# q and k of a two-layer graph network made for two pairs of batches at once

## The chip, the cores and the metric

The kernel runs on one core of one Trainium2 chip. The metric is the device time of one execution in microseconds, the median of several runs. One further execution is recorded by the hardware profiler; all views of the profile shown here come from it.

## The reference

x has 128 batches of 128 nodes with 512 features; adj is one 128 x 128 matrix of zeros and ones. Two layers follow each other, each with a residual and a normalisation of rows. All is float32.

```python
# layer 0: attention with 8 heads of 64, masked by adj
q, k, v = x @ Wq + bq, x @ Wk + bk, x @ Wv + bv
scores = einsum('bqhd,bkhd->bhqk', q, k) / 8 + (1 - adj) * -1e9
out = einsum('bhqk,bkhd->bqhd', softmax(scores), v)
x = layernorm(x + out @ Wo + bo)
# layer 1: graph attention
h = x @ W
e = leaky_relu((h @ a1)[:, :, None] + (h @ a2)[:, None, :], 0.2) * adj
x = layernorm(x + elu(softmax(e) @ h + beta * h))
```

## The kernel before

**Groups and products.** Two batches make a group, 64 groups in all (G = 2, NG = 64). Each of the five products with a 512 x 512 weight (q, k, v, w for Wo, h for W) is made for a whole group by a Strassen-like scheme: the weight and the pair of batches are cut into blocks of 256, seven block products replace eight, and sums of blocks are formed before and after. `product(name, g, n)` issues block product n (1 to 7); `weight_sum` forms the sums of weight blocks once, at the start; `block_sum(name, g, n)` forms the four differences of x blocks on POOL, for each group. Products 1, 6, 5 and 3 accumulate in one region of PSUM, product 2 has its own, and 7 and 4 share a third. `take_part` moves a region out of PSUM, `add_block` adds one on VectorE. A product that continues a region must wait until the region was read by the step before it: 4 waits for the add of 7.

**Shapes.** In v, w and h a block of x is stationary and 256 columns of the weight move (line 298). In q and k (line 304) the weight block is stationary and 128 columns, the nodes of one batch, move; so a q or k product is 4 matmuls of 128 columns and a v, w or h product 2 of 256. Each float32 matmul has two records in the profile, so these are 8 and 4 records.

**One group's way.** `fetch_blocks` loads x in blocks of 32 rows, `turn_x` transposes it on VectorE into xT (once for each batch of the group), then `block_sum`, the products of q, k and v, `scores` on TensorE, `mask` and `row_max` on VectorE, `exps` and `normalise` on ScalarE. `attn_write` and `attn_read` carry the weights of attention through DRAM in blocks, `turn_attn` transposes them on VectorE, `attend` multiplies with v, `attend_evict` adds v's bias. w's products follow, with x (read again by `fetch_x`, with bo added by `residual` on POOL) as residual. The second layer is alike but smaller: `wa_column` computes W a for both halves of a on VectorE, once at the start; `edge`, `leaky`, `edge_exp` and `weights` make its attention; `aggregate` and h's products end it, with `elu_max`, `elu_exp` and `elu_sum`, and `norm_f` and `store`.

**Order.** Nothing is left to a scheduler. Every call is a piece with a place, a number near its due time in microseconds from a plan. All pieces are sorted by place and issued in that order, so that each engine's queue and SP's DMA queue have a fixed order and wait in it. `rows(g)` holds one group's places; group g adds g * STEP. The table `other` has places of their own for the first and last groups, and `last_rows` has the end, in which the last group's work is cut in halves (`end_product`, `end_max`, `end_sum`, `end_stats`) and w is made plainly. Engines wait by semaphores for what they need, so a place is an order and no fixed time.

**Start.** x of group 0, then Wq, Wk and Wv are loaded through SP. `load_later` issues five small loads on POOL: bv, beta, the halves of a (each spread over 128 partitions), bo. `keep_busy` runs matmuls on the identity until work arrives. `wa_column` needs W and a.

**Buffers.** PSUM is a pool of eight tiles of one bank. xT and the differences tx have two buffers (groups alternate), qT and kT one, v two.

Of the kernel before, what the change touches and what calls it, by code (L numbers as in the profile page):

```python
# [13 lines left out]
P = 128  # L14
# [4 lines left out]
STEP = 36.678  # L19
# [3 lines left out]
def gnn_two_layers(  # L23
# [54 lines left out]
    def load_blocks(g):  # L78
        t = grp.tile([P, G, 4, P], F32, tag="xb", name=f"xblk_{g}", bufs=1)
        for a in range(4):  # L80
            (nc.scalar if g == 0 and a >= 2 else nc.sync).dma_start(
                out=t[a * Q : (a + 1) * Q].rearrange("r t b d -> r (t b) d"),
                in_=x[g * G : (g + 1) * G, :, a * P : (a + 1) * P].rearrange(
                    "t (b r) d -> r (t b) d", r=Q
                ),
            )
        return t
# [25 lines left out]
    xblk, xn = {0: load_blocks(0)}, {}  # L113
# [23 lines left out]
    keep_busy(15, "early")  # L137
# [92 lines left out]
    xT, right, tx, qT, kT, vb, y, hp, main, side, oT, zT, xr = ({} for _ in range(13))  # L230
    BIAS = {"q": bq_c, "k": bk_c}
    OUT = {"q": qT, "k": kT, "v": vb, "w": y, "h": hp}

    def turn_x(g, t):
        if t == 0:
            xT[g] = grp.tile([P, NC, G * N], F32, tag="xT", name=f"xT_{g}")
        nc.vector.transpose(  # L237
            xT[g][:, :, t * N : (t + 1) * N].rearrange("p m (b r) -> p b m r", r=Q),
            xblk[g][:, t].rearrange("p b (c m) -> p b m c", c=Q),
        )  # L240

    def block_sum(name, g, n):

        if name == "x":
            b11, b12 = xT[g][:, :2, :N], xT[g][:, :2, N:]
            b21, b22 = xT[g][:, 2:, :N], xT[g][:, 2:, N:]
        else:
            src = oT if name == "w" else zT
            b11, b12 = src[g * G][:, :2], src[g * G + 1][:, :2]
            b21, b22 = src[g * G][:, 2:], src[g * G + 1][:, 2:]  # L250
        if (name, g) not in tx:
            tx[name, g] = grp.tile(
                [P, 4, 2, N], F32, tag=f"t{name}", name=f"t{name}_{g}", bufs=2 if name == "x" else 1
            )
        t1, t2, t3, t4 = (tx[name, g][:, i] for i in range(4))
        to, a, b = {1: (t1, b12, b11), 2: (t2, b22, t1), 3: (t3, b22, b12), 4: (t4, b21, t2)}[n]
        nc.gpsimd.tensor_tensor(to, a, b, ALU.subtract)  # L257
        right[name, g] = {1: b11, 2: b21, 3: b22, 4: t4, 5: t1, 6: t2, 7: t3}

    def first_blocks(name, g):  # L260

        if (name, g) in right:
            return right[name, g]
        if name == "x":
            return {1: xT[g][:, :2, :N], 2: xT[g][:, 2:, :N]}
        src = oT if name == "w" else zT
        return {1: src[g * G][:, :2], 2: src[g * G][:, 2:]}

    def region(name, g, n):

        if n in (7, 4):
            return side[name, g]
        return main[name, g][:, 1 if n == 2 else 0]

    def product(name, g, n):
        first = False
        if n == 1:
            main[name, g] = ps_mm.tile([P, 2, HF], F32, tag="mm", name=f"p{name}_{g}")
            first = True
        if n == 7:  # L280
            if name == "k":
                side["k", g] = side["qk", g][:, 1]
            else:
                t = ps_mm.tile([P, 2, HF], F32, tag="mm", name=f"e{name}_{g}")
                side["qk", g] = t
                side[name, g] = t[:, 0]
                first = True


        out = region(name, g, n)  # L290
# [4 lines left out]
        b = first_blocks(name if name in "wh" else "x", g)[n]  # L295
        if name in "vwh":
            for c in range(2):
                nc.tensor.matmul(  # L298
                    out, b[:, c, :], a[:, c, :], start=first and c == 0, stop=(c == 1), skip_group_check=True,
                )  # L300
        else:
            for m in range(2):
                for c in range(2):
                    nc.tensor.matmul(  # L304
                        out[:, m * N : (m + 1) * N], a[:, c, m * P : (m + 1) * P], b[:, c, :],
# [4 lines left out]
    def block(name, g, i, j):  # L310

        out = OUT[name]
        if name in "qk":
            if g not in out:
                out[g] = grp.tile([P, NC, G * N], F32, tag=name, name=f"{name}T_{g}", bufs=1)
            return out[g][:, 2 * i : 2 * i + 2, j * N : (j + 1) * N]
        return whole(name, g * G + j)[:, i * HF : (i + 1) * HF]

    def whole(name, b):
        out = OUT[name]  # L320
        if b not in out:
            out[b] = wk2.tile([P, D], F32, tag=name, name=f"{name}_{b}")
# [18 lines left out]
    def take_part(name, g, n, i, j):  # L341
# [8 lines left out]
        else:  # L350
            for m in range(2):
                nc.scalar.activation(  # L352
                    dst[:, m, :], src[:, m * N : (m + 1) * N], AF.Identity,
# [3 lines left out]
    def add_block(name, g, n, i, j):  # L357

        src, dst = region(name, g, n), block(name, g, i, j)
        if name in "qk":  # L360
            src = src.rearrange("p (m n) -> p m n", m=2)
# [5 lines left out]
    def scores(b):  # L367
# [4 lines left out]
        rows = slice(i * N, (i + 1) * N)  # L372
        for m in range(HP):
            for j in range(2):
                feats = slice(j * HD, (j + 1) * HD)
                nc.tensor.matmul(  # L376
                    psc[b][j][:, m, :], qT[g][feats, m, rows], kT[g][feats, m, rows],
# [360 lines left out]
    def rows(g):  # L738

        b0, b1 = g * G, g * G + 1  # L740
        return (
            (-44.347, fetch_blocks, g), (-35.5, turn_x, g, 0), (-35.24, turn_x, g, 1),
            (-33.234, block_sum, "x", g, 1), (-29.664, block_sum, "x", g, 2),
            (-28.037, block_sum, "x", g, 3), (-27.486, block_sum, "x", g, 4),
            (-24.602, product, "q", g, 1), (-22.912, take_part, "q", g, 1, 0, 0),
            (-17.846, product, "k", g, 1), (-17.044, take_part, "k", g, 1, 0, 0),
            (-16.821, product, "q", g, 2), (-16.581, product, "q", g, 6),
            (-13.839, product, "k", g, 6), (-13.188, product, "k", g, 2),
            (-12.987, take_part, "q", g, 6, 1, 0), (-12.001, product, "q", g, 7),
            (-11.879, add_block, "q", g, 2, 0, 0), (-11.237, product, "k", g, 7),  # L750
            (-10.614, product, "q", g, 5), (-10.426, add_block, "k", g, 2, 0, 0),
            (-9.421, take_part, "k", g, 6, 1, 0), (-8.361, take_part, "q", g, 5, 1, 1),
            (-7.18, product, "k", g, 5), (-5.626, fetch_x, b0),
            (-5.405, take_part, "k", g, 5, 1, 1), (-5.039, product, "q", g, 3),
            (-4.941, add_block, "q", g, 7, 1, 1), (-4.893, add_block, "k", g, 7, 1, 1),
            (-4.838, product, "k", g, 3), (-4.757, residual, b0),
            (-3.456, take_part, "k", g, 3, 0, 1), (-3.441, take_part, "q", g, 3, 0, 1),
            (-0.228, product, "q", g, 4), (0.123, fetch_x, b1), (0.161, product, "k", g, 4),
            (0.517, add_block, "k", g, 4, 1, 0), (1.111, add_block, "q", g, 4, 1, 0),
            (2.487, scores, b0), (3.199, scores, b1), (4.193, mask, b0, 0),  # L760
            (4.492, product, "v", g, 1), (4.517, mask, b0, 1), (4.517, row_max, b0),
            (4.641, mask, b1, 0), (5.302, take_part, "v", g, 1, 0, 0), (5.86, exps, b0, 0),
            (6.834, residual, b1), (7.227, product, "v", g, 6), (7.65, product, "v", g, 2),
            (7.788, exps, b0, 1), (8.282, mask, b1, 1), (8.312, exps, b0, 2),
            (8.356, row_max, b1), (9.38, exps, b0, 3), (9.64, product, "v", g, 7),
            (9.91, add_block, "v", g, 2, 0, 0), (10.078, take_part, "v", g, 6, 1, 0),
            (10.336, row_inv, b0), (10.432, normalise, b0, 0), (10.446, normalise, b0, 1),
            (10.513, normalise, b0, 2), (11.118, product, "v", g, 5), (12.165, normalise, b0, 3),
            (12.283, exps, b1, 0), (12.823, attn_write, b0), (16.179, exps, b1, 1),
            (17.177, exps, b1, 2), (17.937, exps, b1, 3), (18.213, row_inv, b1),  # L770
            (20.003, normalise, b1, 0), (20.463, normalise, b1, 1), (21.094, normalise, b1, 2),
            (21.248, normalise, b1, 3), (21.546, attn_read, b0), (21.948, turn_attn, b0, 0),
            (22.433, attn_write, b1), (23.511, take_part, "v", g, 5, 1, 1),
            (24.964, product, "v", g, 3), (26.507, turn_attn, b0, 1),
            (27.155, add_block, "v", g, 7, 1, 1), (27.181, attn_read, b1),
            (30.486, product, "v", g, 4), (31.193, take_part, "v", g, 3, 0, 1),
            (31.929, turn_attn, b1, 0), (32.334, turn_attn, b1, 1),
            (32.982, add_block, "v", g, 4, 1, 0), (36.883, attend, b1), (38.699, attend, b0),
            (39.543, attend_evict, b0), (39.643, attend_evict, b1),
            (40.299, block_sum, "w", g, 1), (40.441, block_sum, "w", g, 2),  # L780
            (41.662, block_sum, "w", g, 3), (42.036, product, "w", g, 1),
            (42.978, product, "w", g, 2), (44, take_part, "w", g, 1, 0, 0),
            (44.174, add_block, "w", g, 2, 0, 0), (45.529, block_sum, "w", g, 4),
            (46.326, product, "w", g, 6), (46.362, product, "w", g, 7),
            (47.112, take_part, "w", g, 6, 1, 0), (47.797, product, "w", g, 5),
            (49.563, take_part, "w", g, 5, 1, 1), (50.272, add_block, "w", g, 7, 1, 1),
# [385 lines left out]
```

## Time and profile before

| | |
|---|---|
| Median of 3 runs | 2380.74 us (2379.07 to 2380.99) |
| The profiled execution | 2381.36 us, its span 2379.6 us, mean granted clock 0.998 |
| TensorE, loads of stationary blocks | 2353.9 us, 2177.3 us (99%, 91% of the span) |
| VectorE, ScalarE, POOL | 1960.5, 1589.5, 867.7 us (82%, 67%, 36%) |
| DMA | 269.83 MB, 113 GB/s on average |
| q and k products (line 304) | 7168 of 17702 matmul records |

A row of the page or of a group list gives line, engine, operation, tiles, count, busy time and mean duration. A row of the timeline gives start and length of a run of like instructions; in brackets stands the idle time before it with what ended it. A row of the stretch table gives a stretch, its length, the busy time of TensorE, its weight loads, VectorE, ScalarE and POOL with the number of instructions, the granted clock, the DMA engines' share and GB/s. Matmuls overlap, so their durations are longer than the distances of their starts. Times are from the span's start.

### The profile page before, as it was taken

To read this page: it belongs to the slowest core of one execution; us is meant where nothing else is said; L and a number is where in the kernel's file an instruction comes from. 1 tells how busy PE (TensorE), PEld (TensorE's weight loads), DVE (VectorE), ACT (ScalarE), POOL (GpSimd) and SP (SyncE) were. 2 spreads that over 40 slices of the span, in tenths; PEclk is the share of its full clock that TensorE was granted. 3 is DMA by queue.
4 is the path that set the end of the run, shared out by engine and by line. 5 is a ranking of instruction groups with operands and counts; after the bars stand their busy time and mean duration, and the time that the engine had idled before them with its cause. 6 is when DMAs were issued, how large, how long until landed. Compare 5 with 4: busy or idle time off the path is not lost.

```text
span 2379.6 us, 50867 instructions
## 1 busy us (share of the span) xinstructions
PE 2353.9 (99%) x17702; PEld 2177.3 (91%) x17702; DVE 1960.5 (82%) x4390; ACT 1589.5 (67%) x5762; POOL 867.7 (36%) x1047
## 2 busy tenths in 40 slices
PE   8999999999999999999999999999999999999997
PEld 7999899999999999999999999999999999999986
DVE  6787788888888888888888888888888888888887
ACT  4675666766766667667666676676666766766765
POOL 6243333433433334334333333343343333433432
PEclk9999999999999999999999999999999999999999
DMA  6333334334333343343433433424434334333432
GB/s 192 107 92 119 111 107 125 95 118 128 97 119 116 105 122 103 109 134 92 120 119 103 122 108 109 127 91 121 123 102 118 110 109 125 96 117 124 114 115 73
DMA packets 256193, 269.83 MB, mean 113 GB/s; under 512 B 57456, under 2 KB 204912, under 8 KB 255552
## 3 DMA queue, kind: packets, MB, share of 16 engines
q1 hardware_dynamic: 254992, 265.45, 37.1%
q8 instruction: 140, 2.29, 0.4%
q0 software_dynamic: 400, 0.86, 0.1%
q14 instruction: 117, 0.96, 0.1%
q10 hardware_dynamic: 544, 0.26, 0.0%
HBM read 157.62 MB, written 108.85 MB: 112 GB/s over the span
## 4 chain that ended last, share of the span: by engine, by line
PE 95%; DMA 2%; DVE 1%; ACT 1%; issue 0%; SPq 0%; POOLq 0%; POOL 0%; ACTq 0%; DVEq 0%
PE pk L304 12%; PE pq L304 12%; PE pv L298 12%; PE ph L298 11%; PE pw L298 11%; PE eq L304 9%; PE psc L376 5%; PE po L451 5%; PE pz L639 5%; PE eh L298 4%; PE ew L298 4%; PE ev L298 4%; DMA w_sb<-in_L_gnn_W_dram 1%; DMA wk_sb<-in_L_gnn_Wk_dram 0%; DMA scr<-sb 0%
## 5 line engine op out<-in xcount | busy, mean ns | idle before, releaser
L432 POOL TENSOR_TENSOR x<-x,bo_b_in 128x512 f32<-128x512 f32 x128 | 163.3, 1277 | 858.6 <-DMA x<-in_x_dram 858.6
L398 ACT ACTIVATE s<-s,nmax 128x128 f32<-128x128 f32 x1024 | 396.9, 396 | 58.3 <-DVE nmax L392 58.2
L412 ACT ACTIVATE sb<-s,rinv 128x128 f32<-128x128 f32 x1024 | 325.2, 392 | 0.4 <-DVE rinv L405 0.4
L352 ACT ACTIVATE kT<-pk,bk_c 128x128 f32<-128x128 f32 x512 | 159.7, 363 | 204.3 <-PE pk L304 146.2
L352 ACT ACTIVATE qT<-pq,bq_c 128x128 f32<-128x128 f32 x512 | 160.1, 367 | 156.7 <-PE pq L304 156.7
L502 DVE SCALAR_TENSOR_TENSOR ya<-w,wa_row 128x512 f32<-128x512 f32 x256 | 223.9, 874 | 4.4
L398 ACT ACTIVATION_READ_ACCUMULATOR s<-s,nmax 128x1 f32 x1024 | 199.2, 195 | 0.0
L463 ACT ACTIVATE oT<-po,bv_c 128x128 f32<-128x128 f32 x512 | 139.1, 382 | 80.2 <-PE po L451 80.1
L349 DVE TENSOR_TENSOR w<-pw,x 128x256 f32<-128x256 f32 x252 | 106.4, 422 | 99.8 <-PE pw L298 94.0
L441 DVE STREAM_TRANSPOSE attnT<-ab 128x512 f32<-128x512 f32 x256 | 172.6, 693 | 7.5 <-DMA ab<-scr 7.2
L384 DVE SCALAR_TENSOR_TENSOR s<-psc,amask 128x512 f32<-128x512 f32 x256 | 168.7, 681 | 0.8 <-PE psc L376 0.8
L392 DVE TENSOR_REDUCE nmax<-s 128x8 f32<-128x1024 f32 x128 | 156.1, 1220 | 4.4
L346 ACT COPY h<-ph 128x256 f32<-128x256 f32 x252 | 93.7, 372 | 94.9 <-PE ph L298 94.7
L346 ACT COPY v<-pv 128x256 f32<-128x256 f32 x256 | 94.4, 369 | 86.4 <-PE pv L298 59.9
L237 DVE STREAM_TRANSPOSE xT<-xblk 128x512 f32<-128x512 f32 x128 | 139.7, 1110 | 6.2 <-DMA xblk<-in_x_dram 6.2
L257 POOL TENSOR_TENSOR tx<-xT 128x256 f32<-128x256 f32 x128 | 95.6, 748 | 124.3 <-PE psc L376 104.3
L654 DVE SCALAR_TENSOR_TENSOR u<-h,x 128x512 f32<-128x512 f32 x126 | 87.1, 691 | 63.7 <-ACT h L346 61.6
L304 PE MATMUL pq<-xT,wq_sb 128*128 128x128 f32 x1024 | 135.1, 275 | 3.0 <-DMA wq_sb<-in_L_gnn_Wq_dram 3.0
L304 PE MATMUL pk<-xT,wk_sb 128*128 128x128 f32 x1024 | 135.9, 277 | 2.1 <-DMA wk_sb<-in_L_gnn_Wk_dram 2.1
L298 PE MATMUL pv<-wv_sb,xT 128*128 128x256 f32 x512 | 137.5, 392 | 0.0
L304 PEld LDWEIGHTS pk<-xT,wk_sb 128*128 128x128 f32 x1024 | 130.2, 193 | 5.5 <-DMA wk_sb<-in_L_gnn_Wk_dram 2.3
L304 PEld LDWEIGHTS pq<-xT,wq_sb 128*128 128x128 f32 x1024 | 129.3, 192 | 6.4 <-issue 3.2
(677 smaller groups left out, 6349.8 us busy)
## 6 DMA issues: line engine op xcount, KB each, us to landing
scr<-sb SPq DMA_DIRECT2D x128, 512.0 KB
ab<-scr SPq DMA_DIRECT2D x512, 128.0 KB
x<-in_x_dram SPq DMA_DIRECT2D x128, 256.0 KB
xblk<-in_x_dram SPq DMA_DIRECT2D x254, 128.0 KB
out_dram<-u SPq DMA_DIRECT2D x126, 256.0 KB
pb<-s2d SPq DMA_DIRECT2D x62, 128.0 KB
attd<-att SPq DMA_DIRECT2D x62, 128.0 KB
ab<-attd SPq DMA_DIRECT2D x248, 32.0 KB
```

Source lines behind the costliest of these rows:

```text
L237: nc.vector.transpose(xT[g][:, :, t * N : (t + 1) * N].rearrange("p m (b r) -> p b m r", r=Q), xblk[g][:, t].rearrange("p b (c m) -> p b m ...
L298: nc.tensor.matmul(out, b[:, c, :], a[:, c, :], start=first and c == 0, stop=(c == 1), skip_group_check=True,)
L304: nc.tensor.matmul(out[:, m * N : (m + 1) * N], a[:, c, m * P : (m + 1) * P], b[:, c, :], start=first and m == 0 and c == 0, stop=(c == 1) ...
L346: nc.scalar.copy(dst, src)
L352: nc.scalar.activation(dst[:, m, :], src[:, m * N : (m + 1) * N], AF.Identity, bias=BIAS[name][:, 2 * i + m : 2 * i + m + 1],)
L384: nc.vector.scalar_tensor_tensor(s_t[b][:, j * HP : (j + 1) * HP, :], psc[b][j], SCALE, amask.rearrange("p (o n) -> p o n", o=1).broadcast ...
L392: nc.vector.tensor_reduce(nmax[b], s_t[b], AX.X, ALU.max, negate=True)
L398: nc.scalar.activation(s_t[b][:, h, :], s_t[b][:, h, :], AF.Exp, bias=nmax[b][:, h : h + 1], accum_out=rsum[b][:, h : h + 1],)
L412: nc.scalar.mul(sb[b][:, :, h, :], s_t[b][:, h, :].rearrange("p (b c) -> p b c", c=Q), rinv[b][:, h : h + 1],)
L432: nc.gpsimd.tensor_tensor(xr[b], xr[b], later["bo"], ALU.add)
L441: nc.vector.transpose(attnT[b].rearrange("p h (a r) -> p a h r", r=Q)[:, rows], ab[b].rearrange("p a (h c) -> p a h c", c=Q)[:, rows],)
L502: nc.vector.scalar_tensor_tensor(z, y[b], 1.0, wa_row[j], ALU.mult, ALU.mult, accum_out=s12[g][:, i, j : j + 1])
```

## The change

q and k are made for two groups (a pair of groups, four batches) by one set of products. xT and the differences of all pairs lie in two fixed tiles, `xT_all` and `xs_all`, in which the even and the odd group are side by side; `x_blocks(None)` gives blocks with 256 columns, `x_blocks(0)` and `x_blocks(1)` the 128 of one group for v. `product` for q and k moves 256 columns and has a PSUM tile for each of its three regions; q's and k's evictions and adds are of that width, and `scores` takes its group's part. v has four buffers.

```diff
-STEP = 36.678
+STEP = 72.624
...
     def load_blocks(g):
-        t = grp.tile([P, G, 4, P], F32, tag="xb", name=f"xblk_{g}", bufs=1)
+        if g == 1:
+
+            t = wk2.tile([P, H, N], F32, tag="attnT", name="xblk_1")
+            t = t.rearrange("p (t b) d -> p t b d", t=G)
+        else:
+            t = grp.tile([P, G, 4, P], F32, tag="xb", name=f"xblk_{g}", bufs=1)
...
-    xblk, xn = {0: load_blocks(0)}, {}
+    xblk, xn = {0: load_blocks(0), 1: load_blocks(1)}, {}
...
-    keep_busy(15, "early")
+    keep_busy(20, "early")
...
+    xT_all = cpool.tile([P, NC, G, 2, N], F32, tag="xT", name="xT")
+    xs_all = cpool.tile([P, 4, 2, 2, N], F32, tag="tx", name="tx")
+
     def turn_x(g, t):
-        if t == 0:
-            xT[g] = grp.tile([P, NC, G * N], F32, tag="xT", name=f"xT_{g}")
         nc.vector.transpose(
-            xT[g][:, :, t * N : (t + 1) * N].rearrange("p m (b r) -> p b m r", r=Q),
+            xT_all[:, :, t, g % 2, :].rearrange("p m (b r) -> p b m r", r=Q),
...
+    def x_blocks(slots):
+        s = slice(slots, slots + 1) if isinstance(slots, int) else slice(0, 2)
+        b = [xT_all[:, 2 * h : 2 * h + 2, j, s] for h in range(2) for j in range(G)]
+        t = [xs_all[:, i, :, s] for i in range(4)]
+        b11, b12, b21, b22, t1, t2, t3, t4 = (a.rearrange("p c s n -> p c (s n)") for a in b + t)
+        return b11, b12, b21, b22, (t1, t2, t3, t4)
...
+    def factor(name, g, n):
+
+        if name in "qkv":
+            b11, b12, b21, b22, (t1, t2, t3, t4) = x_blocks(g % 2 if name == "v" else None)
+            return {1: b11, 2: b21, 3: b22, 4: t4, 5: t1, 6: t2, 7: t3}[n]
...
+        if name in "qk":
+            return (two if n == 2 else main)[name, g]
...
-                        out[:, m * N : (m + 1) * N], a[:, c, m * P : (m + 1) * P], b[:, c, :],
+                        out[:, m, :], a[:, c, m * P : (m + 1) * P], b[:, c, :],
...
-                out[g] = grp.tile([P, NC, G * N], F32, tag=name, name=f"{name}T_{g}", bufs=1)
-            return out[g][:, 2 * i : 2 * i + 2, j * N : (j + 1) * N]
+                out[g] = grp.tile([P, NC, G, 2, N], F32, tag=name, name=f"{name}T_{g}", bufs=1)
+            return out[g][:, 2 * i : 2 * i + 2, j].rearrange("p m s n -> p m (s n)")
...
-        rows = slice(i * N, (i + 1) * N)
+        qs, ks = (t[g - g % 2][:, :, i, g % 2, :] for t in (qT, kT))
```

All places are new: `rows` has one list for even groups, which also makes q and k for the pair, and one for odd groups, which has only v; a pair g // 2 adds (g // 2) * STEP. Of the new lists the parts that the steps below speak of (the whole has some 160 pieces a group):

```python
# even group
(-29.134, product, "k", g, 1), (-28.828, product, "q", g, 1), (-28.51, product, "k", g, 2),
...
(0.747, scores, b0), (0.767, scores, b1),
...
(19.288, product, "v", g, 3),
...
(25.91, normalise, b1, 3),
...
(31.237, attn_write, b1), (33.268, attn_read, b0), (33.385, attn_read, b1), (33.851, turn_attn, b0, 0),
(34.469, turn_attn, b0, 1), (34.976, turn_attn, b1, 0), (35.624, turn_attn, b1, 1),
(36.826, attend, b0), (36.846, attend, b1),
# x of the next even group: places -48.877 and -42.022 of turn_x, one STEP on 23.7 and 30.6
# odd group
(-38.159, fetch_blocks, g), (-36.754, turn_x, g, 0), (-34.832, turn_x, g, 1),
...
(34.39, product, "v", g, 4),
...
(61.056, normalise, b1, 3),
```

At the start the order changes as well. On POOL `load_later` moves from ahead of all work to behind v's weight sums, and on VectorE `wa_column` stands between the adds of product 2 and those of product 7:

```diff
-    at(0.583, load_later)
-    at(5.685, load_k_and_v)
+    at(-1.685, load_k_and_v)
...
+    at(11.013, weight_sum, "v", 3, nc.gpsimd)
+    at(12.293, weight_sum, "v", 1, nc.gpsimd)
+    at(13.573, weight_sum, "v", 2, nc.gpsimd)
+    at(14.853, weight_sum, "v", 4, nc.gpsimd)
+    at(16.133, load_later)
+    at(16.198, wa_column, 1, 1)
+    at(16.928, wa_column, 0, 2)
+    at(17.658, wa_column, 0, 3)
+    at(18.388, wa_column, 0, 1)
+    at(19.118, wa_column, 1, 2)
+    at(19.848, wa_column, 1, 3)
```

There the first pair's products on TensorE stand in the order q 1, 7, 2, k 1, 7, 6, 2, q 6, k 5, q 5, k 3, q 3, q 4, k 4, v 1, scores. VectorE has k's add 7 at place 20.578, q's add 7 at 21.963, q's add 4 at 26.008 and k's at 27.743. SP has x of batches 0 and 1, Wo and W1 (the second layer's weight) behind Wv; before, W1 stood ahead of Wo. At the end `last_rows` gives the last two batches' four `end_product` calls first and then, behind them on VectorE, all of `end_max`, `end_sum` and `end_stats`.

## Prediction

> **What bounds the kernel now.** I read the page's busy times, then the stretch table of two groups, TensorE's timeline, and last the start and the end.
>
> ```profile
> PE 2353.9 (99%) x17702; PEld 2177.3 (91%) x17702; DVE 1960.5 (82%) x4390; ACT 1589.5 (67%) x5762; POOL 867.7 (36%) x1047
> ...
> 1036.57:1073.07 36.50, 36.50 (x278) 33.92 (x277) 30.44 (x71) 24.80 (x90) 13.27 (x16) 1.00 0.37 113
> 1073.07:1109.57 36.50, 36.50 (x278) 33.92 (x276) 30.40 (x70) 24.81 (x90) 13.28 (x16) 1.00 0.37 113
> ```
>
> Two stretches from scores to scores are both 36.50 us with TensorE busy throughout, while VectorE has 6 us free and ScalarE 12. Now the timeline inside one:
>
> ```profile
> 1042.11 1.03 PE L298 MATMUL pv<-wv_sb,xT 128*128 128x256 f32 x4
> ...
> 1046.43 1.03 PE L298 MATMUL pw<-wo_sb,tw 128*128 128x256 f32 x4
> ...
> 1067.51 1.05 PE L304 MATMUL pq<-xT,s_q 128*128 128x128 f32 x8
> ...
> 1070.19 1.06 PE L304 MATMUL eq<-tx,wk_sb 128*128 128x128 f32 x8
> ```
>
> Starts, not durations, give the price. Five products of 4 records with 256 columns lie between 1042.11 and 1046.43: 0.864 us each, 216 ns a record. Three products of 8 records with 128 columns lie between 1067.51 and 1070.19: 0.893 us each, 111.6 ns a record. A column is dearer in the narrow form, and TensorE has no gap that anything else could fill. Ahead of this steady part stands a start of some 30 us, behind it an end that waits on chains.
>
> **What the skill says.** "Perfetto Trace Analysis", section Identifying the Most-Contended Engine, warns that matmul busy share says little of headroom; hence starts. "TensorE: Matmul & The Clock Gate", section Back-to-back issue gap, gives N/2.4 + 2.5 ns a matmul, so wider ones share a fixed cost. The trace agrees in direction: two narrow records take 223.2 ns, a wide one 216; 7.2 ns saved, which I use.
>
> **Part 1, wide products.** Now 14 q and k products a group, 28 a pair of groups, 28 x 0.893 = 25.0 us. After: 14 a pair, each 8 records of 256 columns, 2 x 0.864 = 1.728, 24.2 us. Saved: 0.812 us a pair, x 32 = **-26.0 us**, all on the engine that sets the time. The bounds are -22 (a wide record at 217.5) and -27.5. Records fall by 3584.
>
> The evictions come along. ScalarE's 1024 biased ones (363 to 367 ns, 128 elements) become 512 of 256; the nearest row, the copy of v, has 369, so ScalarE loses some 130 us of work. VectorE's 384 adds at 0.42 become 192 of 128x512, like the mask's 0.68: -30 us. Both lie beside TensorE and are costed at nothing; were that cover gone, they would only help. The transposes and POOL's subtractions keep sizes and number.
>
> **Part 2, one xT for all pairs.** xT and its differences lose their second buffer: the transposes of the next pair wait for this pair's v products. In the new list v even ends at 19.3, its slot is turned at 23.7; v odd ends at 34.4, its slot is turned from 35.9. First readers are the next k and q products 1, behind scores and one w product: 3.9 us of TensorE after attend starts. The late transposition (1.1 us, behind two adds of 0.42 and the load) is done some 2 us after it. I cost this at nothing, 0 to 0.3 us a pair. PSUM: q and k hold six of eight tiles, seven live at most in either order.
>
> **Part 3, the tighter chain in mid-pair.** The even group's attention of its second batch goes out to DRAM and back between normalise and attend. Two rows of the chain at the start, SP's and TensorE's timelines in the steady part:
>
> ```profile
> 42.02 2.63 DMA scr<-sb
> ...
> 45.98 3.22 DMA ab<-scr
> ...
> 1058.74 0.34 SPq L419 DMA_DIRECT2D scr<-sb  x1
> ...
> 1071.17 1.97 PE L451 MATMUL po<-attnT,v 128*64 128x128 f32 x32
> ```
>
> Write 2.63, issue of the earlier reads 1.3, last read 3.22, two transposes 1.29: 8.5 us needed; before there are 12.4 (1058.74 to 1071.17). In the new list, from normalise (25.91) to that attend stand ten v and h products (8.6 us) and one attend (0.97): 9.6 us, **1.1 us of slack**. The odd group has six wide products, an aggregate and an attend, 12.2 us. If the chain holds, cost 0.
>
> **Part 4, the start.** TensorE's timeline of the first 31 us, two rows of the stretch table (last columns: clock, DMA share, GB/s), and a row of the DMA list (last number: us from issue to landing):
>
> ```profile
> 11.20 1.13 PE L304 MATMUL pq<-xT,wq_sb 128*128 128x128 f32 x8 [3.00 <-DMA wq_sb<-in_L_gnn_Wq_dram]
> ...
> 30.46 0.72 PE L376 MATMUL psc<-kT,qT 64*128 64x128 f32 x8
> ...
> 8.00:10.00 2.00, 0.20 (x2) 0.01 (x1) 0.00 (x0) 0.94 (x1) 1.84 (x4) 1.00 0.56 139
> ...
> 18.00:20.00 2.00, 2.00 (x12) 2.00 (x11) 1.25 (x3) 0.43 (x2) 0.00 (x0) 0.50 1.14 192
> ...
> uf_in<-in_L_gnn_a_dram POOLq DMA_DIRECT2D x2, 256.0 KB, 10.8
> ```
>
> Scores start at 30.46 after 16 products (14.3 us): 16.2 us of start are not products. The small loads of POOL (two uf_in among them) share the engines with Wq: 139 GB/s in 8 to 10 us against 420 at 12. "DMA: Bandwidth & Descriptors", section SWDGE vs HWDGE vs iDMA, says that each DMA engine takes turns between the two kinds; this stretch agrees. Moved away, they let Wq (behind 0.5 MB more of x, some 2 us) land near 10, and four transposes at 1.07 from 5.4 end at 9.7: first product near 10.3.
>
> But the new list puts load_later behind v's four sums, and wa_column(1, 1) on VectorE right after the second add, ahead of q's and k's adds 7 and 4. Wv comes fifth, near 16.5; four sums at 1.3 end at 21.7; a's second half is the fourth POOL load, issued by 24, and lands 10 to 11 later: **34.5**. Behind the waiting wa_column stand five more (0.73 each, to 38.8) and the adds of 7 for k and q (40.0). Product q 4 writes the tile that the add reads, so TensorE, done with q 3 at 31.1, waits 9 us. Then q 4, k 4, an add, v 1: scores at 44.5, and 2 us more for a throttled clock. The page on TensorE, section What's actually happening, says that about 3.4 us of idleness halve the clock; the trace's 0.50 at 18 to 20 us follows an idle stretch. So scores start near 46.5 after 25.1 us of products (14 wide, one v): 21.4 us of start, **+5.2 us** against 16.2. Bounds: -5 (a lands with W1, near 24, and nothing waits) and +9. The five DMAs of load_later (bv, beta, two of a, bo; 2.9 us of issuing on POOL from 4.0 now) then hold up POOL's block sums 4 from 21.7 to 24.6, and residual waits for bo (14.2 us to landing, so about 38); q 4 at 40 covers the first, the late scores the second. On SP the x loads now pass W1 and Wo, and Wo passes W1: W1 lands near 24 by bytes (6.5 MB at 290 KB a us), before a. Five more warm-up matmuls end before the first product.
>
> **Part 5, the end.** Now the last matmul ends at 2372.0 and the span at 2379.6. In the new list all 12 halves of max, sum and stats of the last two batches come after the last product on VectorE: 12 x 0.40, then aggregates, pow (0.55), shift and norm, about 7 us where 4.3 stand now (2371.09 to 2375.39): +2.7; with other waits of a deeper end **+3.5 us**, from 0 to +8. The first groups' change of order (three waits of 0.8 to 1.1 near 220 to 242 now) I leave as it is.
>
> **Sum.** The profiled execution took 2381.4 us around its span of 2379.6: 2381.4 - 26.0 + 5.2 + 3.5 = 2364.1. The three runs' median is 0.6 lower, so **2364 us**, 0.7% less. A measurement of this kernel can tell about 0.2% (4.8 us) from no change.
>
> **Rivals.** (a) The start costs nothing: the loads land early or wa_column waits for W1 alone. Then -5 instead of +5.2: 2354. For it: 10.8 us includes a crowded start. Against: the same engines carry W1 and Wo then. (b) Small waits: some tile, add or transposition is 0.2 to 0.6 us late in each pair, against slacks of that size; +6 to +19, near 2376. For it: the many close neighbours in the list; against: 6 us of free VectorE time a group, and a period that repeats to 0.01 us in the two stretches. (c) **Slower**: the attention chain of part 3 misses attend. If normalise ends 2.4 us later than its place among the products, 1.3 us are lost in each of 31 pairs, +40: 2404. It decides from 1.1 + 17/31 = 1.65 us of lateness on. For it: slack falls from 3.9 to 1.1, and two x loads stand ahead of the write in SP's queue; against: ScalarE gets 4 us a pair lighter. (d) Wide q and k records are no cheaper per column: 2390. Against: the same shape runs in v, w and h at 216 ns.
>
> **How the numbers follow.** Forecast, 2358 to 2372: 0.58. (a) 2352 to 2358: 0.13. (b) 2372 to 2384: 0.12, a quarter of it under 2376. (c) 0.13, (d) 0.04. Faster by over 0.2%: 0.58 + 0.13 + 0.03 = 0.74; within 0.2%: 0.09; slower: 0.17. The range from 2354 to 2383 leaves out (c), (d) and some of (a).
>
> **What would show it.** Right: 14128 matmul records, about 72.2 us from one pair's first scores to the next; q and k products of 1.73 us; a VectorE wait for uf_in ending near 34; scores at 44 to 48. Wrong: a period over 72.7 us with attend waiting for attnT (c), k product 1 waiting for xT (b), or starts of wide records 223 ns apart (d); scores before 40 would mean (a).

## The result, and the profile after

| | before | after |
|---|---|---|
| Median of 4 runs each, same chip | 2380.86 us | 2395.05 us (2393.45 to 2401.01) |
| Ratio after / before | | 1.0064, 95% interval 1.0045 to 1.0083 |
| The profiled execution, its span | 2381.36, 2379.6 us | 2396.14, 2394.4 us |
| Scores of group 0 start | 30.46 us | 46.73 us |
| One pair of groups, scores to scores, mean of the 28 pairs from group 4 to 60 | 73.14 us (73.00 from group 8 on) | 73.12 us |
| Last matmul's end to the span's end | 7.6 us | 10.9 us |

The change makes the kernel slower by 0.64%, where 0.7% faster was forecast. The page's busy times and the stretch table of two pairs, each cut at the scores of its even and odd group (columns as before: busy time of TensorE, weight loads, VectorE, ScalarE, POOL, then clock, DMA share, GB/s):

```profile
PE 2345.2 (98%) x14128; PEld 2046.3 (85%) x14128; DVE 1930.9 (81%) x4198; ACT 1494.2 (62%) x5250; POOL 886.9 (37%) x1047
...
1118.08:1155.10 37.02, 36.57 (x222) 31.73 (x221) 28.49 (x67) 23.09 (x83) 11.05 (x13) 1.00 0.41 108
1155.10:1191.18 36.08, 36.08 (x222) 31.89 (x220) 31.34 (x64) 23.54 (x82) 16.17 (x19) 1.00 0.38 118
1191.18:1227.98 36.80, 36.58 (x223) 31.73 (x221) 28.47 (x66) 23.04 (x83) 11.04 (x13) 1.00 0.40 108
```

TensorE's busy time is 8.7 us less, and it is no longer busy throughout. The half from the odd group's scores to the even group's, which holds the q and k products, repeats to 0.01 us at 36.08. The other half is 36.77 to 37.48, another length in each pair: something ends late in it. TensorE's timeline across the seam shows both:

```profile
1152.59 1.09 PE L469 MATMUL po<-attnT,v 128*64 128x128 f32 x16
1154.08 1.09 PE L469 MATMUL po<-attnT,v 128*64 128x128 f32 x16 [0.39 <-DVE attnT L459]
1155.10 2.06 PE L394 MATMUL psc<-kT,qT 64*128 64x128 f32 x32
...
1158.05 1.89 PE L322 MATMUL p1k<-xT,wk_sb 128*128 128x256 f32 x8
1159.78 1.89 PE L322 MATMUL p1q<-xT,wq_sb 128*128 128x256 f32 x8
```

Wide q and k products start 1.73 us apart, as forecast. The attend of the even group's second batch comes 1.49 us after the first's, and the two take 2.51 us (1152.59 to 1155.10) where the odd group's two take 1.89 (1189.29 to 1191.18): 0.62 lost. The chain of waits, followed back from there (start, length, what), and SP's row behind the write:

```profile
1142.56 1.18 ACT sb L430 x4
...
1143.76 3.97 DMA scr<-sb
...
1149.04 3.46 DMA ab<-scr
...
1152.62 1.32 DVE attnT L459 x2
```

```profile
1144.18 5.30 SPq L442 DMA_DIRECT2D ab<-scr  x8
```

From normalise's end (1143.74) to attend (1154.08) the trip takes 10.3 us. The write alone takes 3.97. Of the eight reads in SP's row the first four fetch the first batch's attention and are issued from 0.4 us behind the write on; the other four, which fetch what the write brings, wait for it.

At the start, TensorE's timeline (two rows), VectorE's (four rows) and POOL's (one row):

```profile
30.33 1.89 PE L322 MATMUL p1q<-xT,s_q 128*128 128x256 f32 x8
40.70 3.51 PE L322 MATMUL p7q<-tx,wq_sb 128*128 128x256 f32 x8 [8.47 <-DVE qT L380]
```

```profile
29.77 1.17 DVE L182 SCALAR_TENSOR_TENSOR wa_t<-w_sb,uf_in 128x512 f32<-128x512 f32 x1 [5.38 <-DMA uf_in<-in_L_gnn_a_dram]
...
30.99 1.65 DVE L182 SCALAR_TENSOR_TENSOR wa_t<-w_sb,uf_in 128x512 f32<-128x512 f32 x1
...
39.27 0.68 DVE L380 TENSOR_TENSOR kT<-p7k,kT 128x512 f32<-128x512 f32 x1
...
46.58 0.68 DVE L182 SCALAR_TENSOR_TENSOR wa_t<-w_sb,uf_in 128x512 f32<-128x512 f32 x1
```

```profile
32.05 1.74 POOL L225 TENSOR_TENSOR s_h<-w_sb 128x512 f32<-128x512 f32 x1
```

The wait for a and the queue behind it are the forecast's, with other parts: a landed 5.7 us after its issue, not 10 to 11, so the wait ended at 29.77; but five of the six wa_columns took 1.62 to 1.65 us, not 0.73. POOL works beside them, on sums of weight blocks and then on residual, until 38.8 us; at 46.58 it is idle. Near the end TensorE waits in two places that before did not have in this size:

```profile
2340.26 3.13 PE L657 MATMUL pz<-attT,x 128*128 128x128 f32 x16 [4.15 <-DVE mv_c L495]
...
2372.43 0.48 PE L644 MATMUL pat<-ident,att 128*128 128x128 f32 x1 [2.20 <-DVE att L638]
2372.70 1.91 PE L686 MATMUL plh<-wk_sb,zT 128*128 128x256 f32 x4
2374.40 1.91 PE L686 MATMUL plh<-w_sb,zT 128*128 128x256 f32 x4
```

Behind the second wait four records take 1.70 us instead of 0.86: half clock until 2377.8.

**Where 14.8 us come from** (2396.14 - 2381.36). Pairs, against the steady 73.00 of before: (73.12 - 73.00) x 28 = +3.4. Start, by the forecast's own rule (46.73 - 25.1 of products, against 16.2): +5.4. The rest, +6.0, lies in the first groups and the end. It is a net figure: before, the pairs from groups 4 and 6 took 74.19 and 75.79 us because of three waits, 4.0 us over the steady pair, and after they take 73.21 and 73.16.

### The profile page after: what moved, and what is told of

It is laid out like the page before. It is cut to its first block, busy times and chain, and to the rows that moved or that the text cites. A ratio compares the mean times of both kernels' runs of the same rounds, so it can differ in the third digit from the quotient of the medians.

```text
span 2394.4 us, 42795 instructions
## 1 busy us (share of the span) xinstructions
PE 2345.2 (98%) x14128; PEld 2046.3 (85%) x14128; DVE 1930.9 (81%) x4198; ACT 1494.2 (62%) x5250; POOL 886.9 (37%) x1047
## 4 chain that ended last, share of the span: by engine, by line
PE 77%; DMA 10%; ACT 4%; DVE 4%; SPq 2%; issue 2%; POOL 0%; DVEq 0%; POOLq 0%; ACTq 0%
PE p1w L315 10%; PE p1q L322 9%; PE p1k L322 9%; PE p1v L315 7%; PE p1h L315 6%; PE psc L394 5%; DMA scr<-sb 5%; PE pz L657 5%; DMA ab<-scr 5%; PE p7q L322 4%; PE p7k L322 4%; PE po L469 4%; PE p7w L315 3%; PE p7v L315 3%; ACT sb L430 3%; PE p7h L315 2%
## 5 line engine op out<-in xcount | busy, mean ns | idle before, releaser
L366 ACT COPY h<-p1h 128x256 f32<-128x256 f32 x252 | 93.0, 369 | 195.0 <-PE p1h L315 176.0
L366 ACT COPY v<-p1v 128x256 f32<-128x256 f32 x256 | 94.8, 370 | 138.5 <-PE p1v L315 138.4
L372 ACT ACTIVATE kT<-p1k,bk_c 128x256 f32<-128x256 f32 x256 | 106.1, 465 | 114.7 <-PE p1k L322 113.0
L369 DVE TENSOR_TENSOR w<-p1w,x 128x256 f32<-128x256 f32 x252 | 103.3, 410 | 79.5 <-PE p1w L315 79.3
L469 PE MATMUL po<-attnT,v 128*64 128x128 f32 x2048 | 133.0, 277 | 12.3 <-DVE attnT L459 12.0
L469 PEld LDWEIGHTS po<-attnT,v 128*64 128x64 f32 x2048 | 111.1, 137 | 39.6 <-issue 37.5
L657 PEld LDWEIGHTS pz<-attT,x 128*128 128x128 f32 x1024 | 130.7, 194 | 10.2 <-DVE mv_c L495 4.5
L657 PE MATMUL pz<-attT,x 128*128 128x128 f32 x1024 | 131.9, 278 | 4.5 <-DVE mv_c L495 4.1
L372 ACT ACTIVATE qT<-p1q,bq_c 128x256 f32<-128x256 f32 x256 | 106.0, 465 | 47.1 <-PE p1q L322 47.1
L394 PE MATMUL psc<-kT,qT 64*128 64x128 f32 x2048 | 132.3, 279 | 0.0
```

Source lines behind the costliest of these rows:

```text
L366: nc.scalar.copy(dst, src)
L372: nc.scalar.activation(dst[:, m, :], src[:, m, :], AF.Identity, bias=BIAS[name][:, 2 * i + m : 2 * i + m + 1],)
L394: nc.tensor.matmul(psc[b][j][:, m, :], qs[feats, m, :], ks[feats, m, :], start=True, stop=True,)
L469: nc.tensor.matmul(po[b][j * HD : (j + 1) * HD, m, :], vb[b][:, h * HD : (h + 1) * HD], attnT[b][:, j * HP + m, :], start=True, stop=True,)
L657: nc.tensor.matmul(pz[b][:, c, :], x1[b][:, c * P : (c + 1) * P], attT[g][:, i, :], start=True, stop=True,)
```

## The experiments

Every experiment is an edit of the changed kernel. Times are compared as ratios to the kernel before on the same chip, and as medians with 2395.05. The runs were made on several chips, on which the median of the kernel before lies between 2379.5 and 2380.9 us, and the intervals of the ratios are 0.1 to 0.2% wide to either side; a difference of two or three us is not told from none. The profiles, one execution each, also differ where no edit touched anything: with the start left alone the first scores come at 46.65 to 48.35 us (six profiles), and with the end left alone group 63's scores stand 68.9 to 73.6 us ahead of the span's end (seven profiles).

**1. The wide products undone.**

```diff
-                    nc.tensor.matmul(out[:, m, :], a[...], b[:, c, :], ...)
+                    for s in range(2):
+                        nc.tensor.matmul(out[:, m, s * N : (s + 1) * N], a[...],
+                                         b[:, c, s * N : (s + 1) * N], ...)
```

> The changed kernel with each q and k product of 8 matmuls of 256 columns cut into 16 of 128, everything else as it is. If wide records are cheaper by 7.2 ns for each pair of narrow ones and TensorE sets the pace in the half of the pair that has these products: that half (36.08 us from the odd group's scores to the next) becomes 36.8 to 36.9, the other stays near 37.0, and the time rises by 24 to 27 us to about 2420. If wide records bring nothing, or the mid-pair chain takes up what they bring: within 5 us of 2395. 17712 or so matmul records.

Measured: 2422.82 us, ratio 1.0184 (1.0168 to 1.0199), 27.8 us over the changed kernel. The stretch table of one pair:

```profile
1133.43:1170.41 36.98, 36.57 (x222) 31.73 (x220) 28.65 (x67) 23.11 (x83) 11.04 (x13) 1.00 0.41 108
1170.41:1207.33 36.92, 36.92 (x334) 35.79 (x332) 31.31 (x64) 23.66 (x82) 16.59 (x19) 1.00 0.38 115
```

The half with the products grows by 0.84 us in every pair, where 0.812 was forecast, and the other hardly moves (37.03 to 37.14 us on average). The records are 17712. So wide records do save what was forecast, and what took the saving back lies elsewhere.

**2. Two moves in SP's queue of each middle pair.** The rows of the even and the odd group:

```diff
-(33.268, attn_read, b0)
+(26.5, attn_read, b0)      # ahead of attn_write b1 at 31.237
...
-(30.3, fetch_x, b1)
+(33.5, fetch_x, b1)        # behind attn_read b1 at 33.385
```

> The changed kernel with two moves in SP's queue in each middle pair: the read of the even group's first attention goes ahead of the write of its second (now behind it), and the odd group's second x load goes behind the reads. Theory (the second attend waits for a trip through DRAM that is slow because the 512 KB of the other batch's read and an x load share the engines with it: write 3.97 us, last read 3.46 us): the write lands in about 2.7 us, the stall ahead of the second attend (0.62 us a pair on average) goes, the mean period falls from 73.06 to 72.3 to 72.5, the time by 16 to 20 us to about 2377. Rival (VectorE's queue is what is late: h's and v's adds and a transposition ahead of the turn): the period stays at 73.0 to 73.1 and the time within 4 us of 2395.

Measured: 2378.49 us, ratio 0.9996 (0.9987 to 1.0004), 16.6 us off. The stretch table, and SP's timeline of the trip:

```profile
1114.41:1150.86 36.45, 36.39 (x223) 31.73 (x221) 28.78 (x67) 22.69 (x82) 11.08 (x13) 1.00 0.35 109
1150.86:1186.94 36.08, 36.08 (x223) 31.89 (x221) 31.49 (x64) 23.83 (x84) 16.23 (x19) 1.00 0.38 117
```

```profile
1140.09 0.34 SPq L437 DMA_DIRECT2D scr<-sb  x1
1142.77 1.75 SPq L442 DMA_DIRECT2D ab<-scr  x4
```

The reads wait for the write, so their issue 2.68 us after it is the write's landing: 2.7 instead of 4.0. The pair takes 72.53 us and repeats to 0.01; no attend waits. The order in VectorE's queue, the rival, was not changed and was not the cause. What still stands between 72.53 and the 72.19 of the forecast is one place in TensorE's timeline:

```profile
1143.32 1.03 PE L315 MATMUL p7h<-s_h,th 128*128 128x256 f32 x4
1144.41 1.13 PE L315 MATMUL p1h<-w_sb,th 128*128 128x256 f32 x4
```

The second row, h's product 5, starts 1.09 us behind the first where 0.864 is the distance, and the product behind it starts 0.96 us later: 0.22 and 0.10 us.

**3. Only the first of the two moves.**

```diff
-(33.268, attn_read, b0)
+(26.5, attn_read, b0)
```

> The changed kernel with only the first of the two moves in SP's queue: the read of the even group's first attention ahead of the write of its second; the x load stays ahead of that write. If the 512 KB of the read beside the write make the trip late, the period falls to 72.5 to 72.6 as with both moves and the time to about 2379. If it is the x load ahead of the write (it waits for an add of w, and its 256 KB share the engines), the period stays at 72.9 to 73.1. Normalise, not the x load, ends last ahead of the write in the trace (1143.72 against 1143.1), so I expect the first.

Measured: 2379.08 us, ratio 1.0000 (0.9992 to 1.0008), 72.53 us a pair. The first move is the whole effect: the other batch's read of 512 KB, issued 0.4 us behind the write, made the write late. With the x load still ahead of it the write lands after 3.02 us (its reads are issued at 1141.82, the write at 1138.80) against 2.68 without, which the slack covers: the pair is the same.

**4. Normalise earlier, SP's order left.**

```diff
-(24.459, normalise, b1, 0), (24.608, normalise, b1, 1), (25.181, normalise, b1, 2), (25.91, normalise, b1, 3),
+(22.05, normalise, b1, 0), (22.1, normalise, b1, 1), (24.2, normalise, b1, 2), (24.4, normalise, b1, 3),
```

> The changed kernel with one move on ScalarE in each middle pair: normalise of the even group's second batch goes ahead of the two copies of zT and of an elu exponential (first half of it ahead of the copies, second half right behind them). Theory of the chain: normalise ends 1.5 to 1.8 us earlier, but in SP's queue the odd group's x load, which waits for an add of w at about 1142.2 of a pair at 1155.1, still stands ahead of the write, so the write gains only 0.6 us: the stall of 0.62 us falls to 0.1 to 0.3, the period to 72.5 to 72.8, the time by 8 to 15 us. Rival (VectorE's queue): no change of the period. Second rival (the copies of zT are needed at once): product h 1 waits for zT by up to 1 us a pair and the time rises by 10 us or more.

Measured: 2384.19 us, ratio 1.0020 (1.0012 to 1.0027), 10.9 us off; 72.72 us a pair on average. In a pair whose first attend starts at 1148.25, normalise ends near 1137.7, but the write is issued at 1138.74, right behind the x load: 9.51 us ahead of that attend, against 8.83 in the changed kernel. So the write gained the 0.6 to 0.7 us that the x load left it. Starting the same trip earlier removes part of the same stall: two ways into the chain, one answer.

**5. The start: six wa_columns later.**

```diff
-at(16.198, wa_column, 1, 1) ... at(19.848, wa_column, 1, 3)    # six, ahead of the adds 7
+at(22.1, ...) at(22.2, ...) at(26.1, ...) at(28.4, ...) at(32.9, ...) at(34.5, ...)
```

> The changed kernel with six wa_columns set behind q's and k's adds 7 instead of ahead of them; nothing else moves. Theory (the start is lost to the queue on VectorE: adds 7 stand behind wa_columns that wait for a's second half and then take 1.65 us each beside POOL): q 4 follows q 3 at about 32.1, the half-clock product is gone, the first scores come at 36.5 to 38 instead of 46.7, and the time falls by 8 to 10 us to 2386 to 2388. Rival (something else holds q 4 or the scores, such as POOL's block sums 4 behind the five small loads): scores stay over 43 and the time is within 3 us of 2395.

Measured: 2390.19 us, ratio 1.0047 (1.0032 to 1.0062), 4.9 us off, where 8 to 10 were expected; the ratio's interval overlaps that of the changed kernel, so it is the place of the scores that decides. They start at 36.36, as the theory has it, but TensorE then runs into the same columns in their new place, ahead of an add of v, with half clock behind the wait until some 51 us, and half the gain is gone:

```profile
47.08 1.60 PE L315 MATMUL p1v<-s_v,xT 128*128 128x256 f32 x4 [3.28 <-DVE v L380]
```

**6. The start: small loads ahead of v's sums again.**

```diff
-at(16.133, load_later)
+at(10.9, load_later)
...
+# two wa_columns stay at 16.198 and 16.928; the others at 22.1, 22.2, 26.1, 32.9, 33.0, 33.018
```

> The changed kernel with POOL's five small loads back ahead of v's four weight sums (behind the last of the first x differences), and of the six wa_columns only two left ahead of q's and k's adds 7, the others in later gaps of VectorE. Theory (what costs the start is the queue behind wa_columns that wait for a and run at 1.65 us beside POOL): a lands before W1 (23.8), the first two wa_columns fill VectorE's idle 24 to 28, the scores come at 36 to 37 as with the columns moved alone, and the wait of 3.3 us of v product 3 for an add behind three more columns falls to about 1: 2 to 4 us faster than that run's 2390.2, so 2386 to 2388. Rival (the early small loads share the engines with Wk and Wv and delay them): v's sums or k's first product start over 1 us later and the gain is lost: 2390 to 2394.

Measured: 2386.54 us, ratio 1.0026 (1.0017 to 1.0035), 8.5 us off. Scores start at 36.56, and v's wait shrinks to 1.09 us. The rival is half right: v's sums start only 0.7 us later, but W1, issued ahead of the small loads but still in flight beside them, lands at 27.9 instead of 23.3, and VectorE now waits for it:

```profile
28.04 0.72 DVE L182 SCALAR_TENSOR_TENSOR wa_t<-w_sb,uf_in 128x512 f32<-128x512 f32 x1 [3.56 <-DMA w_sb<-in_L_gnn_W_dram]
```

**7. The tail in another order.**

```diff
+end_max, end_sum, end_stats of (b0, 0), (b0, 1); end_aggr b0; (b1, 0); end_norm, end_store b0; then (b1, 1)
-(88.926, norm_f, b0)                # batch 124; was behind aggregate_evict b1 of the last group
+(87.0, norm_f, b0)
-(83.366, weights, g, 1)
+(82.4, weights, g, 1)
```

> The changed kernel with another order at the very end: the max, sum and statistics of the last two batches' halves in the order in which their products end (first the first batch's, whose normalisation then runs beside the last product), batch 124's normalisation a step earlier, and the last batch's attention weights ahead of elu_max of batch 125. Theory (the tail of 10.9 us from the last matmul's end to the span's end is 12 VectorE halves kept behind the last product): the tail falls to 6 to 7.5 us, TensorE's last wait (2.20 us for att) falls to about 0.9 and the half-clock stretch behind it shrinks: 5 to 7 us off, about 2389. Rival (the tail is bound by the stores of batches 124 and 125, whose buffers the last two take, or by ScalarE): the tail stays over 9.5 us and the time within 2 us of 2395.

Measured: 2395.12 us, ratio 1.0057 (1.0042 to 1.0073): no gain. VectorE's and TensorE's timelines:

```profile
2382.15 0.42 DVE L697 SCALAR_TENSOR_TENSOR u<-plh,x 128x256 f32<-128x256 f32 x1 [2.98 <-DMA out_dram<-u]
```

```profile
2380.54 1.13 PE L686 MATMUL plh<-wk_sb,zT 128*128 128x256 f32 x4 [1.21 <-ACT zT L664]
```

The last batches take the buffers of 124 and 125, so end_max waits for their stores: the rival, though the tail falls a little more than it had it, from 10.9 to 9.2 us. The wait for att is 0.80 as expected, but the earlier normalisation now stands ahead of a copy of zT on ScalarE, and TensorE waits 1.21 for that. From group 63's scores to the end this profile takes 68.8 us, 4.1 less than the changed kernel's; but experiments 2, 3 and 6, which leave the end alone, take 68.9 to 69.0, so the new order itself is worth some 0.2 us at most. The start and the first groups, which the edit leaves alone too, took 3.7 us longer in this execution.

**8. Three repairs together** (6, 2 and 7).

> The changed kernel with three repairs together: the start (small loads early, four wa_columns later), SP's order in mid-pair, the order of the tail. If the three losses are separate they add up: 2395 - 8 - 16.6 - 5.5, so 2363 to 2367, period 72.53. If they overlap (an earlier start meets a late load, the earlier end meets a store): 2368 to 2374.

Measured: 2368.46 us, ratio 0.9948 (0.9936 to 0.9961): 0.5% faster than the kernel before. The forecast of 2363 to 2367 counted 5.5 us for the tail, which brought nothing alone. The two repairs that worked add up to 25.1 us; 26.6 were found, the same within the intervals.

**9. Two more waits.** To the three repairs, for the odd group in each pair, and for group 61:

```diff
-(31.137, product, "v", g, 3)
+(30.45, product, "v", g, 3)         # ahead of h's product 5 at 30.506
...
-107.021, 113.369, 113.648, 114.079, 114.538, 115.153, 116.439, 116.538, 117.009, 117.679, 109.739, 120.059, 124.478,
+107.021, 109.4, 109.45, 109.5, 109.55, 112.4, 113.95, 113.96, 113.97, 114.0, 109.739, 118.2, 121.25,   # edge ... weights_turn
```

> The same with two more: v's product 3 of the odd group ahead of h's product 5 of the even one (which waits 0.22 us in each pair for an add that follows a ScalarE copy), and group 61's edge scores, weights and their transpose earlier (TensorE waits 4.15 us there near the end). If both waits are what they look like: period 72.3 and 27 x 0.22 = 6 us, the end 1.5 to 4 us: 2354 to 2359. Rival: the add or the turn of attnT is only late for the next in line, the period stays at 72.5 and the gain is under 3 us.

Measured: 2385.49 us, ratio 1.0021 (1.0013 to 1.0028), 17 us worse than the three alone. TensorE's timeline in the pair:

```profile
1139.43 1.13 PE L315 MATMUL p1v<-s_v,xT 128*128 128x256 f32 x4
1140.40 1.03 PE L315 MATMUL p1h<-w_sb,th 128*128 128x256 f32 x4
1141.89 1.13 PE L315 MATMUL p1h<-s_h,zT 128*128 128x256 f32 x4 [0.46 <-ACT h L366]
```

Product 5 no longer waits, but product 3 now follows it directly and waits for the copy of product 5: v's product had been the distance between the two. The pair takes 73.04 us, 0.5 x 28 = 14 us in all. The other 4 us are at the end: the wait of 4.15 us turns into 1.34 for pz and 3.14 at the attend behind it, whose attention is read from DRAM only from 2329.52 on and turned at 2334.46, and half clock follows.

**10. The three repairs, and h's add 2 ahead of the copy of h's product 6.**

```diff
-(103.113, add_block, "h", g, 2, 0, 0)
+(102.25, add_block, "h", g, 2, 0, 0)     # ahead of take_part h 6 at 102.323, behind product h 6 at 102.218
```

> The three repairs (start, SP's order, tail) with one more on VectorE in each middle pair: the even group's add of h's product 2 goes ahead of ScalarE's copy of product 6 in the written order, so that it waits for product 2 and the first copy alone. In the trace it waits for the copy of product 6 (0.56 us), and product h 5 behind it waits 0.22 us on TensorE with 0.10 us of a slower restart. If that is the whole of what keeps the period at 72.53: 72.2, and 29 x 0.32 = 9 us off 2368.5, so 2358 to 2361. Rival (the wait moves to the next product, as it did when v's product 3 was moved): period 72.5 or more, 2367 to 2375.

Measured: 2369.37 us, ratio 0.9958 (0.9944 to 0.9971), 72.56 us a pair: the rival. VectorE's and ScalarE's timelines:

```profile
1133.29 0.42 DVE L380 TENSOR_TENSOR h<-p1h,h 128x256 f32<-128x256 f32 x1 [0.57 <-PE p1h L315]
```

```profile
1133.74 0.37 ACT L366 COPY h<-p1h 128x256 f32<-128x256 f32 x1 [1.88 <-DVE h L380]
```

The add, which stands behind product 6 in the written order, now waits for product 6 itself and the copy for the add. The wait has changed its engine, not its length. An add ahead of product 6 was not tried.

## Why the prediction was wrong, by its own steps

**Part 1 (-26.0 us): right.** Products of 1.73 us and 14128 records are there, and the undoing cost 0.84 us a pair in the half that holds them (27.8 us in all, 28.6 by the ratios). Rival (d) falls. The lower bound was summed wrongly: records of 217.5 ns give -20.6, not -22. The formula of "TensorE: Matmul & The Clock Gate", section Back-to-back issue gap, which the page gives for an isolated matmul, would have put 55.8 ns on 128 columns, where a record takes 111.6, and 2.5 ns on what two narrow records lose; the trace's 7.2 ns was the right one to use. Of the work beside TensorE, VectorE lost 29.6 us (30 forecast), ScalarE 95 instead of 130: the biased eviction of 256 columns takes 465 ns on average, where the nearest row, a copy without bias, gave 369. It costs nothing here.

**Part 2 (0): right.** No first product of k or q waits for xT.

**Part 3 (0): the step that failed.** The 8.5 us needed were put together from a trip seen alone: write 2.63, last read 3.22. In the new order the first batch's read is issued right behind this write, so both carry 512 KB at once, and the trip takes 10.2 us. The slack of 1.1 us was counted well: 1.1 - 1.7 = -0.6 us, and 0.59 is what experiments 2 and 3 give back (73.12 - 72.53). With the neighbour moved, the trip from the write's issue to the last landing is 6.9 us and the sum of part 3 holds. So it is the missed attend of rival (c), at 0.6 us instead of 1.3 and with another reason: not a late normalise or the x loads, but a read of its own kind, which SP's list showed ahead of the run. 0.59 x 28 = 17 us.

**Rival (b), which stood at 12%, came on top.** The other 0.34 us a pair (72.53 against 72.19): h's product 5 waits 0.22 us for an add behind a ScalarE copy, and the product behind it starts 0.10 us late. Experiments 9 and 10 moved this wait and did not remove it, so what it hangs on (three engines take turns on one PSUM tile, with one product between them) is read from the trace and not shown by a run. (b) and (c) together, 0.93 us a pair, are more than the 0.81 of part 1; over 28 pairs they are 26 us.

**Part 4 (+5.2 us): right in sum, by luck: two errors cancel.** Scores at 46.73 (46.5 forecast; 46.65 to 48.35 in six profiles), q 4 at half clock. But a landed at 29.75, not 34.5: 10.8 us to landing belonged to a crowded start, and the text had said so under rival (a). Nor did moving the small loads away help Wq: the first product starts at 11.27 us, not 10.3, and before it was 11.20; this did not enter the sum, since VectorE came last. And a wa_column was priced at 0.73 us, its row alone. "SBUF — State Buffer", section SBUF: two separate sides, says that a VectorE operation with two inputs from SBUF and a GpSimd operation that reads SBUF exclude each other on a shared pair of ports. The trace agrees: 1.62 to 1.65 us beside POOL's operations, 0.68 at 46.58 with POOL idle. The prediction left this out. Experiments 5 and 6 bring the scores 10 us forward and give 4.9 and 8.5 us back.

**Part 5 (+3.5 us): the mechanism of the tail was right, the rest of the end was sized too small, and a gain was left out.** The tail grew by 3.3 us (2.7 forecast). In front of it stand the two waits of 4.15 and 2.20 us with half clock behind them, which "other waits of a deeper end" priced at 0.8. The first groups and the end cost 6.0 us more than before although four pairs' saving of 3.2 us falls in them: 9.2. An estimate parts this: with each record of TensorE at the distance of starts of its form (111.6 ns for 128 columns, 216 for 256), the stretch from group 60's scores to the end holds 157.0 us of work before and 149.7 after, and takes 175.0 and 179.3 us. So the end loses 11.6 us more than before. The first groups ahead of group 4 lose 1.6 more, and the three waits that the prediction left as they were are gone, 4.0 us back: 11.6 + 1.6 - 4.0 = 9.2. The row ahead of pz shows attT's transposition late in VectorE's queue; what makes it late was not settled, and moving group 61's weights forward (experiment 9) only shifted the wait.

**The sum.** 2364.1 + 26 (part 3 and rival b) + 0.2 (start) + 5.7 (end, first groups: 9.2 for 3.5) = 2396.0, the profiled time. It closes because the last term is what was left over. The median lay 12 us above the range's end because (b) and (c) had been taken as alternatives, each with its own chance, and not as terms that can both come, and because the end was sized too small.

## What to carry to other kernels

Price a transfer in the queue where it will stand: list what is issued in the microseconds beside it, and take its landing from a row with the same company; the trip put together from times seen alone was 1.7 us too short here. When a change shortens the engine that sets the time by 0.8 us in a 73 us loop, every slack of the same size is a term of the sum, not a rival: add them up. A wait that looks small can be what a spacer in the order still hides; ask what stood between two steps before moving it.

## What the runs showed of the hardware

A 512 KB write to DRAM landed after 2.68 us alone (experiment 2), 3.02 us with a 256 KB load just ahead of it (experiment 3), and 3.97 us with a 512 KB read issued 0.4 us behind it (the changed kernel). VectorE's product with two SBUF inputs took 1.62 to 1.65 us beside POOL's operations and 0.68 alone; one kind of POOL's sums (line 225) rose from 1.28 to 1.74. The loads of a through POOL landed 5.7 us after their issue in the changed kernel, 10.8 in the crowded start of the kernel before; put earlier, in experiment 6, the small loads had a 1 MB weight land 4.6 us later.

How long TensorE waits does not alone decide whether its clock is halved. Near the end, behind waits of 0.52 and 0.35 us, it waits 1.35 us for att in five profiles. Half clock follows in experiments 1 and 4, none in experiments 2, 3 and 6, with the same three waits. TensorE's timeline of experiment 4:

```profile
2361.02 0.33 PE L644 MATMUL pat<-ident,att 128*128 128x128 f32 x1 [1.35 <-DVE att L638]
...
2362.57 1.91 PE L686 MATMUL plh<-w_sb,zT 128*128 128x256 f32 x4
```

Behind the waits of 2.20 us (the changed kernel) and 2.10 us (experiment 5) half clock follows too. From group 63's scores to the end the four profiles with half clock there take 71.4 to 73.6 us, the three without 68.9 to 69.0.
